# Two-layer graph network on one core: eight node tiles taken by counts in place of seven

## The chip, the cores and the metric

The kernel runs on one core of one Trainium2 chip. The metric is device time of one execution in microseconds (us); the time before is the median of three runs. The core's engines are TensorE (PE; its weight loads are shown apart as PEld), VectorE (DVE), ScalarE (ACT), GpSimd (POOL) and the DMA queues. SP's queue and ACT's queue issue plain DMAs, POOL's queue issues the gathers.

## The reference

Two layers of a graph network over 6250 nodes and 100000 edges, then a residual and a layer norm. The edges are sorted by their destination, and the destinations crowd at low node numbers (6250 times the square of a uniform number), the sources are uniform.

```
x: (6250, 256) f32;  src, dst: (100000,), sorted by dst
agg(h) = (1 + eps) * h + segment_sum(h[src], dst, 6250)
h   = relu(relu(agg(x) @ W1a + b1a) @ W1b + b1b)      # (6250, 512)
y   = relu(agg(h) @ W2a + b2a) @ W2b + b2b            # (6250, 256)
out = layernorm(x + y)
```

## The kernel before, in words

Nodes are cut into 49 tiles of 128, edges into 784 chunks of 128 in the order of their destination. A tile's sum over its edges is made in one of two ways.

**By gathers.** For each chunk POOL issues one indirect DMA (line 461) that fetches the 128 source rows into a piece buffer (early; in layer 2 early and late), with room for 24 chunks in layer 1 and 24 in the two buffers of layer 2. PE sums a chunk onto 32 destination slots with a one-hot matrix sel (L954). Chunks form groups; a group's sums are copied out of their bank by ACT (split, L982 in layer 1, L990 in layer 2), put in place by a matmul with a second one-hot matrix (L1001) and added to the tiles' sums by DVE (acc, L1011). Groups are walked from the highest nodes down.

**By counts.** The lowest tiles have the most edges. For these (HEAVY, seven in both layers) layer 1 makes a table of how often each source occurs for each destination. A chunk's one-hot pair is built by DVE (ca at L1523, cb at L1532), multiplied by PE (L1571) and added to the table `at` at a position taken from the data (L1594). The table holds four tiles at a time (RING) in a ring. Tiles are handled in passes of two, the highest first. When a pass's counts are complete, ACT casts each tile's counts for each range of four source tiles to a matmul operand (cf, L1415), casts them once more to 16-bit integers (ci, L1423) and writes these to DRAM from its own queue (counts, L1428) for layer 2. A pass reads all of x again, 13 ranges of it (raw), in two halves for precision (xh: ACT L1385 and L1392, DVE L1394), and PE multiplies counts with both halves at once, 49 products of 512 columns for each tile (L1457). A ring slot that is used again is cleared by ACT (L1437) first. Layer 2 loads the counts (ci, SP's queue, L1243), casts them (cf, L1255), halves the rows of h1 (upper and xr, L1220, L1221, L1225) and makes two products for each of the 49 source tiles and each counted tile (L1331); DVE adds them up (L1274).

**Dense part.** A block of one or two complete tiles is transposed by PE (L1047), copied to zt by ACT (L1059), multiplied by the layer's first matrix (L1086), passed through a relu by ACT (ht, L1096), and multiplied by the second (L1115). Layer 1 then adds the bias (DVE, L1125), takes a relu (ACT, L1127) and writes h1 to DRAM from ACT's queue (L1128). Layer 2 adds x and the bias, normalizes (L1135 to L1158) and writes the output. The gathers of layer 2 read h1, so the first of them waits for the last write of layer 1.

**What sets the order.** Inside a layer the program is emitted by a planner: an event simulation in Python with a cost for each step, a queue for each of PE, DVE and ACT, and priorities (sums of gathered rows first, the dense part and products after them). Its outcome is a fixed order of instructions on each engine. At run time each engine keeps that order and waits by semaphores. How many tiles are counted, how many chunks, the counting steps, the passes and the groups all follow from HEAVY:

```
HEAVY = (7, 7)
...
NC, taken = counted(N, E, HEAVY[0])
STEPS, END, PASSES, FREE = steps(N, E, taken, HEAVY[0])
NC2 = counted(N, E, HEAVY[1])[0]
groups, lo, hi = (a + b for a, b in zip(places(N, E, NC2, NC), places(N, E, NC, NCH)))
...
assert tiles <= 2 * RING
```

Before both layers, a short part loads the edge lists, derives slots and masks, and tests bounds that the plan assumed about the data. One flag decides between this ordered path and a general one; the times here are of the ordered path.

Of the kernel before, what the change touches and what calls it, by code (L numbers as in the profile page):

```python
# [21 lines left out]
SLOTS = 32  # L22
BURST = 4
PIECES = 6
HEAVY = (7, 7)
RING = 4
W = 10
RANGE = 4
# [39 lines left out]
def counted(N, E, tiles):  # L68

    def node(e):
        return N * min((e + deviation(e, E)) / E, 1.0) ** 2

    total = 0
    while (
        node((total + PARTS) * P) < tiles * P
        and span(N, E, (total + PARTS) * P, P, SIGMAS) <= W
    ):  # L80
        total += PARTS
    taken, at = [], 0
    for n in (8, 4, 2, 1):
        a = at
        while at + n <= total and span(N, E, (at + n) * P, n * P, SIGMAS) <= W:
            at += n
        if at > a:
            taken.append((a, at, n))
    return total, taken


def steps(N, E, taken, tiles):

    def reached(c):
        return N * min((c * P + deviation(c * P, E)) / E, 1.0) ** 2

    def begun(c):
        return N * max((c * P - deviation(c * P, E)) / E, 0.0) ** 2

    todo = sorted(((c, n) for a, b, n in taken for c in range(a, b, n)), reverse=True)  # L100
    end = [
        max(i for i, (c, n) in enumerate(todo) if reached(c + n) >= t * P) for t in range(tiles)
    ]
    passes = [tuple(range(t, max(t - PAIR, -1), -1)) for t in range(tiles - 1, -1, -PAIR)]
    if JOINED and len(passes[-1]) < PAIR:
        passes[-2:] = [passes[-2] + passes[-1]]
    free = [
        next((i for i, (c, n) in enumerate(todo) if begun(c) < ts[-1] * P), len(todo))
        for ts in passes
    ]  # L110
    return todo, end, passes, free


def places(N, E, c, chunks):

    def node(e, side):
        return N * min(max((e + side * deviation(e, E)) / E, 0.0), 1.0) ** 2

    groups, lo, hi = [], [], []
    while c < chunks:
        n = min(GRP, -(-(chunks - c) // PARTS) * PARTS)
        while n > PARTS and (
            span(N, E, (c + n) * P, n // PARTS * P, SPREAD, 1) > SLOTS
            or span(N, E, (c + n) * P, n * P, SPREAD, 1) > P
        ):  # L130
            n -= PARTS
        groups.append((c, n // PARTS))
        lo.append(int(node(c * P, -1)) // P)
        c += n
        hi.append(min(int(node(c * P, 1)), N - 1) // P)
    return groups, lo, hi
# [200 lines left out]
def tile_gin_residual_layernorm(  # L337
# [44 lines left out]
    NCH = -(-E // P)  # L382
# [4 lines that stand above are left out]
    assert NC2 <= NC and HEAVY[1] <= HEAVY[0]  # L387
    groups, lo, hi = (a + b for a, b in zip(places(N, E, NC2, NC), places(N, E, NC, NCH)))
    NG = len(groups)
    BEGIN = (next(g for g in range(NG) if groups[g][0] == NC), 0)  # L390
    SAME = HEAVY[0] == HEAVY[1]
    assert SAME or lo[BEGIN[0]] >= HEAVY[1]
    NCP = groups[-1][0] + PARTS * groups[-1][1]
# [1495 lines left out]
```

## Time and profile before

| | us |
|---|---|
| median of three runs | 1335.6 (1334.89 to 1339.82) |
| the profiled execution's own time | 1333.73 |
| its span, first to last instruction | 1332.0 |
| layer 1, up to the first gather from h | 676.63 |
| layer 2, from there to the end of the span | 655.4 |

The rows of the profile give for a group of instructions the busy time, the mean duration in ns and then the idle time just before them with what ended it. A timeline row gives start, duration, engine, line and the instruction, with its idle time in brackets. A stretch row gives length, busy time by engine with the number of instructions, the granted TensorE clock (1.00 is full), the share of the DMA engines and GB/s. Records of pipelined matmuls overlap, so what a matmul costs is taken from the distance between starts.

### The profile page before, as it was taken

Reading aid. Unit: us, or ns where it says so; the run is one execution under the profiler, and the core shown is the slowest. Engines: PE = TensorE matmul, PEld = TensorE weight load, DVE = VectorE, ACT = ScalarE, POOL = GpSimd, SP = SyncE. Lnnn points to the kernel's source line nnn. Section 1 sums busy time; section 2 is a strip of 40 time slices with the busy share of each in tenths; the row PEclk is TensorE's granted clock in tenths of the full one; section 3 lists DMA queues with packets and bytes.
Section 4 is the critical chain, followed back from the end, with each engine's and each line's share of the span. In section 5 each row is a group of like instructions: output and inputs, shape, how many; then the busy total and the mean of one; then the engine's idle time right before and its main releaser. Section 6 shows DMA issues by size and latency. Waiting matters only on the chain. (4 is left out here: it accounts for less than half of the span.)

```text
span 1332.0 us, 18717 instructions
## 1 busy us (share of the span) xinstructions
PE 1171.7 (88%) x6027; PEld 756.0 (57%) x6027; DVE 872.8 (66%) x2031; ACT 603.2 (45%) x1118; POOL 963.8 (72%) x1002
## 2 busy tenths in 40 slices
PE   2379888999899999878759899999989999999986
PEld 1145554655454655444436667767667766677755
DVE  7689888697897787323127668777756655653443
ACT  0213677767675763454255354334334433432222
POOL 6877777777777777777457677777777777777770
PEclk8589999999999999968879899999989999999999
DMA  3635666667676775566669889888889999877782
GB/s 103 189 119 178 182 219 198 207 199 227 207 225 188 219 239 170 151 211 193 198 228 333 296 268 310 252 278 287 289 271 309 301 310 301 289 244 240 242 244 69
DMA packets 160860, 305.72 MB, mean 230 GB/s; under 512 B 25672, under 2 KB 93150, under 8 KB 160754
## 3 DMA queue, kind: packets, MB, share of 16 engines
q0 software_dynamic: 63232, 194.31, 47.2%
q1 hardware_dynamic: 75110, 84.23, 19.3%
q10 hardware_dynamic: 22412, 25.89, 5.6%
q8 instruction: 51, 0.84, 0.3%
q14 instruction: 55, 0.45, 0.1%
HBM read 273.90 MB, written 30.44 MB: 228 GB/s over the span
## 5 line engine op out<-in xcount | busy, mean ns | idle before, releaser
L461 POOL DMA_INDIRECT early<-in_x_dram,srcs x494 | 488.9, 990 | 158.9 <-issue 127.4
L461 POOL DMA_INDIRECT early<-h,srcs x250 | 239.8, 959 | 101.4 <-issue 58.8
L461 POOL DMA_INDIRECT late<-h,srcs x244 | 232.5, 953 | 77.6 <-issue 60.2
L1011 DVE SCALAR_TENSOR_TENSOR acc<-bank,mask,acc 128x256 f32<-128x256 f32 (+1 forms) x368 | 212.8, 607 | 39.4 <-PE bank L1001 34.8
L1086 PE MATMUL bank<-zt,w2a_s 128*128 128x256 f32 (+2 forms) x864 | 181.8, 366 | 7.7 <-DVE acc L1011 6.5
L1115 PE MATMUL bank<-w1b_s,ht 128*128 128x512 f32 (+1 forms) x392 | 184.7, 599 | 1.1 <-DVE acc L1011 0.8
L1086 PEld LDWEIGHTS bank<-zt,w2a_s 128*128 128x128 f32 x864 | 154.8, 195 | 30.4 <-DVE acc L1011 6.9
L954 PE MATMUL bank<-early,sel 128*32 128x256 f32 (+1 forms) x1488 | 134.3, 475 | 32.7 <-DMA early<-h,srcs 15.3
L1331 PE MATMUL bank<-upper,cf 128*128 128x512 f32 (+1 forms) x343 | 149.2, 435 | 13.9 <-ACT upper L1220 13.5
L1331 PE MATMUL bank<-xr,cf 128*128 128x512 f32 (+1 forms) x343 | 138.2, 403 | 0.8 <-DVE xr L1225 0.8
L1594 DVE TENSOR_TENSOR at<-bank,at 128x490 f32 x174 | 115.9, 666 | 28.2 <-ACT cf L1415 14.7
L907 DVE TENSOR_TENSOR sel<-iota,slot 128x256 f32<-128x256 f32 (+2 forms) x116 | 50.6, 436 | 123.5 <-PE bank L954 119.5
L1086 PE MATMUL bank<-zt,w1a_s 128*128 128x256 f32 (+2 forms) x432 | 103.2, 389 | 13.7 <-ACT zt L1059 10.4
L1001 PE MATMUL bank<-split,to 128*128 128x256 f32 (+2 forms) x340 | 100.0, 415 | 15.6 <-ACT split L987 8.7
L1115 PEld LDWEIGHTS bank<-w1b_s,ht 128*128 128x128 f32 (+1 forms) x392 | 73.3, 191 | 70.8 <-issue 58.6
L1457 PE MATMUL bank<-xh,cf 128*128 128x512 f32 (+1 forms) x343 | 104.1, 440 | 8.7 <-DVE xh L1394 8.6
L1255 ACT CAST cf<-ci 128x512 fp32r<-128x512 uint16 (+1 forms) x91 | 53.8, 595 | 121.4 <-PE bank L1331 104.3
L1096 ACT ACTIVATE ht<-bank,b2a_s 128x256 f32<-128x256 f32 (+2 forms) x108 | 44.6, 451 | 139.5 <-PE bank L1086 137.0
L954 PEld LDWEIGHTS bank<-early,sel 128*32 128x32 f32 x1488 | 40.0, 112 | 113.4 <-issue 80.2
L1571 PE MATMUL bank<-cb,ca 128*128 128x490 f16 x288 | 87.6, 381 | 16.1 <-DVE at L1594 10.5
L1115 PE MATMUL bank<-w2b_s,ht 128*128 128x256 f32 (+1 forms) x392 | 101.5, 390 | 0.0
L1086 PEld LDWEIGHTS bank<-zt,w1a_s 128*128 128x128 f32 x432 | 81.9, 207 | 32.7 <-ACT zt L1059 14.9
(138 smaller groups left out, 1650.7 us busy)
## 6 DMA issues: line engine op xcount, KB each, us to landing
raw<-in_x_dram SPq DMA_DIRECT2D x48, 512.0 KB, 4.5
h<-h1r ACTq DMA_DIRECT2D x48, 256.0 KB, 2.5
xr<-h SPq DMA_DIRECT2D x12, 1024.0 KB, 7.3
counts<-ci ACTq DMA_DIRECT2D x84, 128.0 KB, 3.4
ci<-counts SPq DMA_DIRECT2D x84, 128.0 KB, 5.0
acc<-h SPq DMA_DIRECT2D x19, 512.0 KB, 7.5
early<-in_x_dram,srcs POOLq DMA_INDIRECT x494
acc<-in_x_dram SPq DMA_DIRECT2D x21, 256.0 KB, 3.9
```

What stands on the lines that cost most here:

```text
L461: nc.gpsimd.indirect_dma_start(out=rows_[:, j, :], out_offset=None, in_=table, in_offset=bass.IndirectOffsetOnAxis(ap=srcs[:, c : c + 1], ...
L907: nc.vector.tensor_tensor(sel[:, :n, :], iota[:, :SLOTS].unsqueeze(1).to_broadcast([P, n, SLOTS]), slot[:, c0 : c0 + n].unsqueeze(2).to_br ...
L954: mm = nc.tensor.matmul(pm[b * SLOTS : (b + 1) * SLOTS], sel[:, c - groups[g][0], :], rows_[:, l, :], start=(c == part[0]), stop=(c == par ...
L1001: nc.tensor.matmul(pu[:, i * width : (i + 1) * width], to[:used], split[:used, l, :], start=(once or l == 0), stop=(once or l == 1),)
L1011: nc.vector.scalar_tensor_tensor(acc[t], pu[:, i * width : (i + 1) * width], mask[:, t - lo[g], g : g + 1], acc[t], op0=ALU.mult, op1=ALU.add,
L1086: nc.tensor.matmul(ph[:, (f - o) * TILES * P : (f - o) * TILES * P + nb], wa[:, k, f * P : (f + 1) * P], zt[:, k, :nb], start=(k == 0), st ...
L1115: nc.tensor.matmul(po[:m], ht[:, f, i * P : i * P + m], wb[:, f, :], start=(f == 0), stop=(f == KH - 1),)
L1255: nc.scalar.copy(cf_token.tile[:, :n, :].rearrange("p k j -> p (k j)"), token.tile[:, : n * P],)
L1331: nc.tensor.matmul(bank[token.number][:, :width], cf[:m, j, :], of[:m, j, :], start=(j == 0 and of is upper), stop=(j == len(ks) - 1 and o ...
L1457: nc.tensor.matmul(bank[tokens[i].number][:, : 2 * width], cf[:m, j, :], xh[:m, j, :, :].rearrange("p a d -> p (a d)"), start=(k == 0), st ...
L1571: mm = nc.tensor.matmul(bank[token.number][:, : NT * W], a.tile[:, c % BATCH, :], b.tile, start=(j == 0), stop=(j == n - 1),)
L1594: nc.vector.tensor_tensor(to, bank[token[0].number][:, : NT * W].rearrange("p (k w) -> p k w", w=W), to, op=ALU.add,)
```

## The change

One constant is changed.

```diff
-HEAVY = (7, 7)
+HEAVY = (8, 8)
```

By the kernel's formulas it has these consequences:

| | before | after |
|---|---|---|
| chunks counted, in steps | 288 in 174 | 308 in 194 |
| chunks gathered, each layer | 494 | 474 |
| groups of gathered chunks | 85 | 83 |
| passes of layer 1 | (6,5) (4,3) (2,1) (0) | (7,6) (5,4) (3,2) (1,0) |
| products in layer 1 (L1457) | 343 | 392 |
| products in layer 2 (L1331) | 686 | 784 |
| writes and loads of counts | 91 | 104 |

The ring of four tiles is used exactly twice. The planner is run anew, so the orders of all engines change. The groups of the high tiles and their gathers stay as they were; what changes most is the end of each layer, shown here at three places.

PE at the end of layer 1. Its last gathered sum (L954) and all that stands behind it up to the end of the layer, before; the bank's number is that of a program's buffer:

```order
L954 MATMUL bank_486<-early,sel 32x256 x8
L1001 MATMUL bank_491<-split,to 128x256
L1047 MATMUL bank_493<-ident,acc 128x128 x2
L1047 MATMUL bank_489<-ident,acc 128x128 x2
L1086 MATMUL bank_488<-zt,w1a_s 128x128 x4
L1086 MATMUL bank_492<-zt,w1a_s 128x128 x4
L1086 MATMUL bank_490<-zt,w1a_s 128x128 x4
L1086 MATMUL bank_487<-zt,w1a_s 128x128 x4
L1115 MATMUL bank_486<-w1b_s,ht 128x512 x2
L1115 MATMUL bank_491<-w1b_s,ht 128x512 x2
L1115 MATMUL bank_486<-w1b_s,ht 128x512 x2
L1115 MATMUL bank_491<-w1b_s,ht 128x512 x2
```

After, from the last gathered sum on, the first part of the same place:

```order
L954 MATMUL bank_480<-early,sel 32x256 x4
L1457 MATMUL bank_483<-xh,cf 128x512 x4
L1457 MATMUL bank_484<-xh,cf 128x512 x4
L1001 MATMUL bank_481<-split,to 128x256
L1115 MATMUL bank_485<-w1b_s,ht 128x512 x2
L1047 MATMUL bank_482<-ident,acc 128x128 x2
L1047 MATMUL bank_478<-ident,acc 128x128 x2
L1115 MATMUL bank_485<-w1b_s,ht 128x512 x2
L1457 MATMUL bank_483<-xh,cf 128x512 x4
L1457 MATMUL bank_484<-xh,cf 128x512 x4
L1086 MATMUL bank_479<-zt,w1a_s 128x128 x4
L1086 MATMUL bank_481<-zt,w1a_s 128x128 x4
```

The products L1457 of the last pass were all ahead of the last gathered sum; now 42 of its 98 stand behind it, and behind the last of these the dense part of tiles 0 and 1.

ACT at the same place. From its last copy of a gathered sum (split, L982) on, before:

```order
L982 COPY split<-bank_486 128x256
L1059 COPY zt<-bank_493 128x2x128
L1059 COPY zt<-bank_489 128x2x128
L1096 ACTIVATE ht<-bank_488,b1a_s 128x128 x2
L1096 ACTIVATE ht<-bank_492,b1a_s 128x128 x2
L1096 ACTIVATE ht<-bank_490,b1a_s 128x128 x2
L1096 ACTIVATE ht<-bank_487,b1a_s 128x128 x2
L1127 ACTIVATE h1r<-h1r 128x512
L1128 DMA h_60<-h1r 128x512
L1127 ACTIVATE h1r<-h1r 128x512
L1128 DMA h_60<-h1r 128x512
```

After:

```order
L982 COPY split<-bank_480 128x256
L1096 ACTIVATE ht<-bank_478,b1a_s 128x128
L1415 CAST cf<-at 128x512
L1385 CAST xh<-raw 128x4x256
L1392 COPY bank_479<-raw 128x512
L1423 CAST ci<-cf 128x512
L1428 DMA counts<-ci 128x512
L1415 CAST cf<-at 128x512
L1392 COPY bank_480<-raw 128x512
L1059 COPY zt<-bank_482 128x2x128
L1059 COPY zt<-bank_478 128x2x128
L1423 CAST ci<-cf 128x512
```

The casts, count writes and halvings of the last five ranges now stand behind the last split, mixed with the last tiles' relus.

PE at the end of layer 2. From its last gathered sum on, before (one more row of L1115 closes it):

```order
L954 MATMUL bank_6025<-late,sel 32x512 x4
L1115 MATMUL bank_6029<-w2b_s,ht 128x256 x2
L1001 MATMUL bank_6031<-split,to 128x512 x2
L1047 MATMUL bank_6026<-ident,acc 128x128 x4
L1047 MATMUL bank_6027<-ident,acc 128x128 x4
L1086 MATMUL bank_6028<-zt,w2a_s 128x128 x8
L1086 MATMUL bank_6024<-zt,w2a_s 128x128 x8
L1086 MATMUL bank_6030<-zt,w2a_s 128x128 x8
L1086 MATMUL bank_6025<-zt,w2a_s 128x128 x8
L1115 MATMUL bank_6029<-w2b_s,ht 128x256 x2
L1115 MATMUL bank_6031<-w2b_s,ht 128x256 x2
L1115 MATMUL bank_6029<-w2b_s,ht 128x256 x2
```

After, the first part from the last gathered sum on:

```order
L954 MATMUL bank_6244<-late,sel 32x512 x4
L1115 MATMUL bank_6245<-w2b_s,ht 128x256 x2
L1086 MATMUL bank_6246<-zt,w2a_s 128x256 x8
L1001 MATMUL bank_6241<-split,to 128x512 x2
L1115 MATMUL bank_6245<-w2b_s,ht 128x256 x2
L1115 MATMUL bank_6247<-w2b_s,ht 128x256 x2
L1331 MATMUL bank_6248<-upper,cf 128x512
L1331 MATMUL bank_6248<-xr,cf 128x512
```

Products of the last range (32 of them) and the dense part of several blocks, which stood ahead of the last gathered sum, now stand behind it.

## Prediction

> **What bounds the kernel now.** I read the page's header and engine totals first, then stretches of time cut where the layers meet, then GpSimd's timeline at both layers' last gathers, and last the engines behind those gathers.
>
> ```profile
> span 1332.0 us, 18717 instructions
> PE 1171.7 (88%) x6027; PEld 756.0 (57%) x6027; DVE 872.8 (66%) x2031; ACT 603.2 (45%) x1118; POOL 963.8 (72%) x1002
> 60.00:551.00 491.00, 444.62 (x2218) 258.11 (x2219) 403.15 (x919) 285.43 (x513) 372.56 (x379) 0.97 0.63 194
> 551.00:652.00 101.00, 76.92 (x345) 42.12 (x344) 28.86 (x54) 49.61 (x88) 75.77 (x80) 0.82 0.68 210
> 652.00:677.00 25.00, 18.16 (x91) 9.79 (x90) 4.04 (x9) 8.98 (x19) 0.37 (x1) 0.98 0.23 81
> 677.00:1302.00 625.00, 591.90 (x3163) 421.66 (x3164) 384.79 (x767) 244.46 (x467) 471.49 (x494) 0.97 0.87 282
> 1302.00:1332.00 30.00, 19.40 (x134) 15.15 (x133) 10.00 (x28) 6.67 (x19) 0.45 (x1) 0.93 0.16 52
> ```
>
> The stretches give, after their length, busy time of PE, weight loads, DVE, ACT and POOL, then the granted clock, DMA share and GB/s. POOL's 471.49 of 625 looks like slack and is none:
>
> ```profile
> 630.17 0.94 POOL L461 DMA_INDIRECT early<-in_x_dram,srcs  x1 [0.30 <-issue]
> 650.16 0.95 POOL L461 DMA_INDIRECT early<-in_x_dram,srcs  x1 [0.30 <-issue]
> 676.63 1.13 POOL L461 DMA_INDIRECT early<-h,srcs  x1 [25.53 <-DMA h<-h1r]
> 1301.50 0.95 POOL L461 DMA_INDIRECT late<-h,srcs  x1 [0.30 <-issue]
> ```
>
> The first two are sixteen gathers apart: 19.99/16 = 1.25 us a gather, 0.95 of it busy and 0.30 issue. In layer 2 the 494 gathers take 1301.50 - 676.63 = 624.9 us, 1.265 each, with no stop. So gathers set the pace of both layers, and PE, 591.90 of 625 busy in layer 2, is nearly full beside them. A layer is therefore its gathers times their period, plus what stands behind the last gather. Layer 1 has 26.5 us there (650.16 to 676.63), layer 2 has 30.5 (1301.50 to 1332.0).
>
> **The change, part by part.** Removed: 20 gathers a layer, 20 x 1.25 = 25.0 us in layer 1 and 20 x 1.265 = 25.3 in layer 2. All of it is on the path, and with the last gather gone earlier, the work behind it is late next. Also removed are 20 gathered sums and two groups' merges a layer; they stood at gather pace, and count at nothing, hidden by the gathers that stay.
>
> Added in layer 1: 20 counted chunks (matmul, two builds, an update of the table), a pass that has two tiles in place of one: 49 product matmuls, 13 more table casts, 13 more casts to ci and 13 writes of counts. Per gather the engine order of PE is unchanged up to the last counts: it holds 288 counted chunks up to gather 406 before, and 308 up to gather 430 now. DVE's and ACT's share of it is priced by the rows
>
> ```profile
> L1532 DVE TENSOR_SCALAR cb<-numbers,spot 128x490 f16<-128x490 f16 x288 | 89.4, 352 | 8.4 <-PE bank L1571 8.3
> L1594 DVE TENSOR_TENSOR at<-bank,at 128x490 f32 x174 | 115.9, 666 | 28.2 <-ACT cf L1415 14.7 <-ACT at L1437 7.4 <-PE bank L1571 1.9
> L1523 DVE TENSOR_TENSOR ca<-numbers,low 128x512 f16<-128x512 f16 x72 | 48.8, 678 | 0.0
> L1437 ACT ACTIVATE at<-at 128x512 uint16<-128x512 uint16 x36 | 22.5, 628 | 8.5 <-DVE at L1594 4.0 <-ACT ci L1423 2.8 <-DVE acc L1011 0.4
> ```
>
> 20 x (0.352 + 0.666) + 5 x 0.678 = 23.8 us of DVE, in 30 us more of that stretch: the density of now (403.15 of 491), so it is hidden; 13 clears of the table, 13 x 0.63 = 8 us, lie in ACT's idle time there. If that cover is gone the counts end later still, a us for a us. So the early part runs at gather pace as now, and the last pass begins about 24 x 1.25 = 30 us later, near 582 in place of the 552.37 below, with 44 gathers left in place of 88. It does not fit: of its 98 products 42 now stand behind the last gather, with 20 dense matmuls of 512 columns where 8 stood.
>
> What paces that tail is ACT, which takes its work in order. After its last copy of a gathered sum (split) it had only the last tiles' relus; now it has 10 casts cf, 10 casts ci and 10 count writes, 5 casts xh, 9 copies of raw, 9 relus, 3 h1r and 2 zt before the last pass is through. The prices:
>
> ```profile
> 552.37 0.62 ACT L1415 CAST cf<-at 128x512 fp32r<-128x512 uint16 x1 [0.28 <-DVE at L1594]
> 553.01 0.62 ACT L1423 CAST ci<-cf 128x512 uint16<-128x512 f32 x1
> 553.66 0.33 ACTq L1428 DMA_DIRECT2D counts<-ci  x1
> 554.03 0.62 ACT L1415 CAST cf<-at 128x512 fp32r<-128x512 uint16 x1 [0.40 <-ACT ci L1423]
> L1385 ACT CAST xh<-raw 128x1024 fp32r<-128x1024 f32 x48 | 50.0, 1043 | 5.8 <-ACT ci L1423 2.5 <-PE bank L1457 1.2 <-ACT h1r L1127 1.2
> L1392 ACT COPY bank<-raw 128x512 f32<-128x512 f32 x96 | 55.8, 589 | 20.4 <-DVE xh L1394 6.5 <-DVE at L1594 6.2 <-ACT h1r L1127 3.6
> L1096 ACT ACTIVATE ht<-bank,b1a_s 128x128 f32<-128x128 f32 x20 | 6.4, 363 | 6.1 <-PE bank L1086 5.7 <-ACT h1r L1127 0.4
> L1059 ACT COPY zt<-bank 128x256 f32<-128x256 f32 x6 | 2.2, 372 | 25.6 <-PE bank L1047 18.9 <-DMA ci<-counts 6.7
> 658.71 0.37 ACT L982 COPY split<-bank 128x256 f32<-128x256 f32 x1 [0.40 <-ACT h1r L1127]
> 672.78 0.63 ACT L1127 ACTIVATE h1r<-h1r 128x512 f32<-128x512 f32 x1 [1.09 <-DVE h1r L1125]
> ```
>
> One tile and range costs 554.03 - 552.37 = 1.66 us of ACT, its DMA issue included. Eight of those are 13.3, the two of the short last range an estimated 2.0; xh 4 x 1.04 + 0.4 = 4.6; raw copies 8 x 0.59 + 0.4 = 5.1; relus 9 x 0.36 = 3.3; h1r 3 x (0.63 + 0.4 of issue) = 3.1; zt 0.7: 32 us without a wait. Between that and 42 (ACT often waits for a bank or a raw load here) I take 35, nearer the bottom, because nothing else competes by then. The last gather is issued at 650.16 - 25.0 = 625.2; the split began 8.55 after it (658.71), so now near 633.7, and the last product comes near 633.7 + 0.4 + 35 = 669. From the split to layer 2's first gather it was 676.63 - 658.71 = 17.9: merge, adds, transposes, two matmul stages, relu, write. The last pass is followed by the same chain, for tiles 0 and 1, and I give it 17.9 too. Layer 2 then starts near 687.0 in place of 676.6: **+10.4 for layer 1**. Ends: +3 (PE is free when the last gather lands, some 4 us earlier, and ACT packs closer) and +18 (42 on ACT).
>
> Moved with it: layer 2's first loads.
>
> ```profile
> 631.67 0.37 SPq L710 DMA_DIRECT2D w2a_s<-in_L_gnn_W2a_dram  x1
> ```
>
> They are issued right behind the last raw load and the last product of layer 1, whose buffers they reuse: 45 us ahead of the first gather now, about 18 then. I cost this at nothing: the chain of 17.9 us hides it, with DMA at 0.23 in 652 to 677. If that cover is too short, up to 6 us.
>
> Added in layer 2: 98 product matmuls, 13 loads of counts and 13 casts on ACT (one tile more per range, on an engine busy 244.46 of 625), 13 adds on DVE (384.79 of 625): at nothing, hidden by PE. PE's order is again alike per gather up to the end, so the added work is found at the end: behind the last gathered sum stand 36 matmuls of L1115 (10 before), 24 of L1086 with 256 columns (0 before), 64 with 128 (32 before), 32 products (0 before) and 24 transposes (8 before). Prices, the chain's rows for groups and PE's own last rows:
>
> ```profile
> 759.92 1.85 PE bank L1331 x8
> 787.97 3.45 PE bank L1086 x16
> 886.84 1.73 PE bank L1115 x8
> 1306.62 1.06 PE L954 MATMUL bank<-late,sel 128*32 128x512 f32 x8
> 1311.22 0.66 PE L1047 MATMUL bank<-ident,acc 128*128 128x128 f32 x4 [1.60 <-DVE acc L1011]
> 1312.40 0.66 PE L1047 MATMUL bank<-ident,acc 128*128 128x128 f32 x4 [0.52 <-DVE acc L1011]
> 1312.90 7.31 PE L1086 MATMUL bank<-zt,w2a_s 128*128 128x128 f32 x64
> 1320.04 3.62 PE L1115 MATMUL bank<-w2b_s,ht 128*128 128x256 f32 x16
> ```
>
> Plain f32 matmuls have two records each, products and transposes one. So a product is 1.85/8 = 0.231 us, L1086 3.45/8 = 0.431 with 256 columns and (1320.04 - 1312.90)/32 = 0.223 with 128, L1115 1.73/4 = 0.433, a transpose 0.50/4 = 0.125. The tail grows by 26 x 0.433 + 24 x 0.431 + 32 x 0.223 + 32 x 0.231 + 16 x 0.125 = 11.3 + 10.3 + 7.1 + 7.4 + 2.0 = 38.1 us, against 25.3 saved: **+12.8 for layer 2**. Ends: +9 (PE reaches the last sum 1306.62 - 1301.50 = 5.1 after its issue, partly by its own queue) and +20 (waits such as the 1.60 and 0.52 recur three or four times).
>
> Sum: 10.4 + 12.8 = +23.2 on the profiled execution's 1333.73 us, or 1357. That execution stands 1.9 under the median of 1335.6, within their spread (1334.89 to 1339.82), so I predict 1357 for the new median as well. About 0.5%, 6.7 us, can be told from no change.
>
> **Rivals.**
> (1) The gathers are the whole bound and the tails are hidden: -25.0 - 25.3 gives 1283. The place is PE's queue behind each last gather; it decides if less than 25 us is added there. For it: POOL never stops. Against it: 38 us counted there in layer 2, and PE with 33 us idle in 625.
> A rule gives the same time: the Trainium skill (Perfetto Trace Analysis, Identifying the Most-Contended Engine) says to work on the engine with the highest occupancy and not to judge PE's headroom by matmul busy time but by weight loads. By that rule POOL's 72% stands over the weight loads' 57% and cutting gathers pays in full; the row of 677 to 1302 agrees on POOL alone, not on room behind it.
> (2) ACT keeps pace and PE sets layer 1's end: 12 more dense matmuls at 0.86 (twice L1115's 0.433 for twice the columns), 42 products at 0.231, 8 of L1086 at 0.431 and 4 transposes: 10.3 + 9.7 + 3.4 + 0.5 = 23.9 for 25.0 saved, so -1.1, and 1333.7 - 1.1 + 12.8 = 1345. Against it: 32 us of ACT alone.
> (3) PE runs at a lower clock in the longer tails:
>
> ```profile
> 634.04 2.05 PE L1086 MATMUL bank<-zt,w1a_s 128*128 128x128 f32 x16 [0.46 <-ACT zt L1059]
> 649.25 3.47 PE L1086 MATMUL bank<-zt,w1a_s 128*128 128x128 f32 x16 [5.47 <-ACT zt L1059]
> ```
>
> The same 16 records took 3.47 behind a gap of 5.47 us and 2.05 without it, and the stretch 551 to 652 ran at 0.82. Layer 2's tail of some 52 us at 0.82 would add 11: 1368. Against it: five blocks of independent work keep PE fed there.
> The Trainium skill (TensorE: Matmul & The Clock Gate, HAM oscillation) warns of PE gaps above about 3.4 us, after which the clock is halved; the two rows agree.
> (4) The input breaks one of the bounds that are tested ahead of the branch, and the general path runs. From the input: the highest node among tile 7's counted chunks is 966, under 1023, and a chunk group spans at most 7, under 9. Excluded.
>
> **How the numbers follow.** Forecast 0.71, rival 1 0.05, rival 2 0.14, rival 3 0.10. Summed ends: +3 + 9 = +12 gives 1346, +18 + 6 + 20 = +44 gives 1378; rivals 2 and 3 lie in or beside these. The two ends of every term do not meet often, so 1342 to 1374. Faster by over 0.5%: rival 1, 0.04. Within 0.5%: 0.07, from rival 2 with a shorter layer 2. Slower: 0.89.
>
> **What would show it.** Last gathers 25 us earlier in layer 1 (near 625) and gathers of layer 2 in 600 us; products L1457 until near 669, with ACT busy and PE waiting between 634 and 669; the first gather from h near 687; PE busy for some 50 us behind the last gathered sum, 13 before; no changed period of gathers. I am wrong if the period rises above 1.27, if L1457 ends before 660, or if work behind the last gathers runs ahead of them.

## The result, and the profile after

The changed kernel takes 1366.9 us, the median of four runs (1364.0 to 1369.0), against 1335.9 for the kernel before on the same chip. The ratio, formed from the fast runs of both kernels and not from these two medians, is 1.0245, with a 95% interval of 1.0220 to 1.0270: slower by 31.0 us. The profiled execution took 1369.04 us, 2.1 above its median, where the profiled one of before stood 1.9 under its own; so the two traces differ by 35.1 us, and the working below is of these 35.1.

The head and the engine totals of the changed kernel's page:

```profile
span 1367.1 us, 19005 instructions
PE 1203.0 (88%) x6106; PEld 779.0 (57%) x6106; DVE 899.2 (66%) x2069; ACT 628.7 (46%) x1168; POOL 932.9 (68%) x962
```

The span cut at the changed kernel's own marks: up to the last counts, the last gather, the last products and the first gather from h of layer 1; then up to four us before the last gather of layer 2, and from the last gathered sum almost to PE's last group (the 9 us between these two are not shown; columns as before: length, PE, PEld, DVE, ACT, POOL, clock, DMA share, GB/s):

```profile
60.00:586.00 526.00, 467.82 (x2304) 263.78 (x2304) 427.15 (x969) 294.47 (x531) 399.19 (x401) 0.96 0.62 188
586.00:634.00 48.00, 39.12 (x192) 23.94 (x193) 12.90 (x25) 32.63 (x58) 36.42 (x39) 0.93 0.69 209
634.00:671.00 37.00, 32.67 (x146) 20.35 (x144) 12.46 (x22) 29.28 (x60) 0.47 (x1) 0.95 0.36 118
671.00:694.20 23.20, 13.76 (x36) 8.16 (x36) 2.66 (x7) 4.67 (x8) 0.00 (x0) 0.79 0.58 181
694.20:1294.00 599.80, 566.48 (x2974) 399.32 (x2975) 377.66 (x740) 242.97 (x455) 449.79 (x470) 0.97 0.86 283
1303.00:1357.00 54.00, 51.34 (x300) 45.13 (x300) 20.20 (x53) 13.22 (x35) 0.00 (x0) 0.97 0.11 35
```

The marks themselves, from the timeline, each row with start, duration, engine, line: the last gather of layer 1, the last split, the last products, the load of layer 2's weights, the last write of h, the first gather from h, a wait, the last gather and the last gathered sum.

```profile
633.52 0.95 POOL L461 DMA_INDIRECT early<-in_x_dram,srcs  x1 [0.30 <-issue]
641.36 0.38 ACT L982 COPY split<-bank 128x256 f32<-128x256 f32 x1 [0.40 <-ACT ci L1423]
669.30 1.26 PE L1457 MATMUL bank<-xh,cf 106*128 106x512 f32 x2 [0.30 <-DVE xh L1394]
671.66 0.37 SPq L710 DMA_DIRECT2D w2a_s<-in_L_gnn_W2a_dram  x1
687.59 0.33 ACTq L1128 DMA_DIRECT2D h<-h1r  x1
694.24 1.21 POOL L461 DMA_INDIRECT early<-h,srcs  x1 [59.78 <-DMA acc<-h]
774.93 1.01 POOL L461 DMA_INDIRECT late<-h,srcs  x1 [7.31 <-PE bank L954]
1298.13 0.94 POOL L461 DMA_INDIRECT late<-h,srcs  x1 [0.30 <-issue]
1303.02 1.06 PE L954 MATMUL bank<-late,sel 128*32 128x512 f32 x8
```

The gathers did end sooner: 633.5 in place of 650.2 in layer 1. But GpSimd then waits 59.8 us for h, where it waited 25.5, and in layer 2 PE, which was busy for 19.40 of the 30 us behind the last gather, is now busy for 51.34 of the 54 us behind the last gathered sum. Layer 1 is 17.6 us longer (694.24 - 676.63), layer 2 is 17.5 longer (672.9 - 655.4).

### The profile page after: what moved, and what is told of

Read it like the earlier page. It is cut to its first block, busy times and chain, and to the rows that moved or that the text cites. A ratio compares the mean times of both kernels' runs of the same rounds, so it can differ in the third digit from the quotient of the medians.

```text
span 1367.1 us, 19005 instructions
## 1 busy us (share of the span) xinstructions
PE 1203.0 (88%) x6106; PEld 779.0 (57%) x6106; DVE 899.2 (66%) x2069; ACT 628.7 (46%) x1168; POOL 932.9 (68%) x962
## 5 line engine op out<-in xcount | busy, mean ns | idle before, releaser
L461 POOL DMA_INDIRECT early<-in_x_dram,srcs x474 | 476.6, 1006 | 154.6 <-issue 121.9
L461 POOL DMA_INDIRECT early<-h,srcs x238 | 228.5, 960 | 132.0 <-DMA acc<-h 59.8
L1086 PE MATMUL bank<-zt,w2a_s 128*128 128x256 f32 (+2 forms) x864 | 184.8, 369 | 11.2 <-DVE acc L1011 7.4
L1115 PE MATMUL bank<-w1b_s,ht 128*128 128x512 f32 (+1 forms) x392 | 185.1, 601 | 2.5 <-DVE at L1594 2.2
L1331 PE MATMUL bank<-upper,cf 128*128 128x512 f32 (+1 forms) x392 | 169.8, 433 | 18.6 <-ACT upper L1220 17.7
L1086 PEld LDWEIGHTS bank<-zt,w2a_s 128*128 128x128 f32 x864 | 155.8, 196 | 40.9 <-DVE acc L1011 7.8
L1331 PE MATMUL bank<-xr,cf 128*128 128x512 f32 (+1 forms) x392 | 157.9, 403 | 0.8 <-DVE xr L1225 0.8
L954 PE MATMUL bank<-early,sel 128*32 128x256 f32 (+1 forms) x1424 | 127.6, 473 | 29.5 <-DMA early<-in_x_dram,srcs 10.3
L1594 DVE TENSOR_TENSOR at<-bank,at 128x490 f32 x194 | 129.3, 666 | 29.1 <-ACT cf L1415 12.7
L1457 PE MATMUL bank<-xh,cf 128*128 128x512 f32 x392 | 112.1, 424 | 6.8 <-DVE xh L1394 4.8
L1394 DVE TENSOR_TENSOR xh<-bank,xh 128x512 fp32r<-128x512 f32 (+1 forms) x100 | 67.4, 675 | 72.6 <-ACT bank L1392 72.5
L1115 PEld LDWEIGHTS bank<-w1b_s,ht 128*128 128x128 f32 (+1 forms) x392 | 73.5, 191 | 72.8 <-issue 59.3
L1001 PE MATMUL bank<-split,to 128*128 128x512 f32 (+2 forms) x332 | 96.9, 412 | 12.4 <-ACT split L987 8.4
L1086 PE MATMUL bank<-zt,w1a_s 128*128 128x256 f32 (+2 forms) x432 | 101.1, 383 | 7.3 <-ACT zt L1059 3.7
L1274 DVE TENSOR_TENSOR acc<-bank,acc 128x512 f32<-128x512 f32 x96 | 65.0, 683 | 62.9 <-PE bank L1331 58.3
L1532 DVE TENSOR_SCALAR cb<-numbers,spot 128x490 f16<-128x490 f16 x308 | 95.7, 354 | 8.8 <-PE bank L1571 8.6
```

Of the source, the lines that this page charges most:

```text
L461: nc.gpsimd.indirect_dma_start(out=rows_[:, j, :], out_offset=None, in_=table, in_offset=bass.IndirectOffsetOnAxis(ap=srcs[:, c : c + 1], ...
L954: mm = nc.tensor.matmul(pm[b * SLOTS : (b + 1) * SLOTS], sel[:, c - groups[g][0], :], rows_[:, l, :], start=(c == part[0]), stop=(c == par ...
L1001: nc.tensor.matmul(pu[:, i * width : (i + 1) * width], to[:used], split[:used, l, :], start=(once or l == 0), stop=(once or l == 1),)
L1086: nc.tensor.matmul(ph[:, (f - o) * TILES * P : (f - o) * TILES * P + nb], wa[:, k, f * P : (f + 1) * P], zt[:, k, :nb], start=(k == 0), st ...
L1115: nc.tensor.matmul(po[:m], ht[:, f, i * P : i * P + m], wb[:, f, :], start=(f == 0), stop=(f == KH - 1),)
L1331: nc.tensor.matmul(bank[token.number][:, :width], cf[:m, j, :], of[:m, j, :], start=(j == 0 and of is upper), stop=(j == len(ks) - 1 and o ...
```

## The experiments

The table has the changed kernel and seven edits of it; an eighth edit, of the kernel before, stands at the end of this section. The edits are shown shortened, some with a comment added. Each kernel was timed beside the kernel before on the same chip, so the ratios are what to compare; where intervals overlap, the marks in the traces decide. To read those, the spread is needed: three kernels have the same layer 1 (the changed kernel, and the experiments on the products of ranges 3 to 9 and of range 0 below). Their last products ended at 670.6, 668.0 and 665.7 us and their first gather from h was issued at 694.2, 691.7 and 689.5: means 668.1 and 691.8, and a difference under some 3 us is no effect.

| kernel | ratio to before, 95% interval | last product ends | first gather from h | last gather | from there to the end |
|---|---|---|---|---|---|
| before | 1 | 631.6 | 676.6 | 1301.5 | 30.5 |
| changed | 1.0245 (1.0220 to 1.0270) | 670.6 | 694.2 | 1298.1 | 69.0 |
| eighth tile in layer 1 alone | 1.0110 (1.0079 to 1.0140) | 664.0 | 687.4 | 1312.7 | 40.1 |
| casts on VectorE | 1.0219 (1.0194 to 1.0245) | 664.0 | 687.3 | 1291.7 | 70.4 |
| casts doubled | 1.0271 (1.0246 to 1.0296) | 676.2 | 699.6 | 1303.2 | 68.2 |
| weights loaded behind h | 1.0229 (1.0199 to 1.0258) | 666.3 | 686.4 | 1289.2 | 67.2 |
| 224 products fewer, early | 1.0218 (1.0181 to 1.0255) | 668.0 | 691.7 | 1292.9 | 71.1 |
| 56 products fewer, at the end | 1.0212 (1.0176 to 1.0249) | 665.7 | 689.5 | 1292.4 | 64.0 |
| 19 gathers fewer in layer 1 | 1.0170 (1.0137 to 1.0202) | 657.1 | 680.2 | 1282.5 | 70.8 |

**The eighth tile in layer 1 alone.**

```diff
-HEAVY = (8, 8)
+HEAVY = (8, 7)
```

> The eighth tile in layer 1 alone: HEAVY = (8, 7), layer 2 takes seven tiles by counts and gathers rows for the rest, as before. Theory (the two layers lose separately, each by its own tail): layer 1 as in the changed kernel, its first gather from h near 694 us, and layer 2 as in the kernel before, 655 us from there to the end, so 1347 to 1354 us, about 16 us under the changed kernel. Rival (the loss is one of the boundary: a layer 1 that ends late starts layer 2 badly, whatever its tiles): layer 2 keeps its longer time, 668 us or more, and the whole stays at 1361 us or above. Second rival (only layer 2 costs anything, layer 1's shift is noise of the schedule): 1336 us.

Measured: 1350.1 us, 15.2 above the kernel before and about half of the 31 us. The first gather from h and the last gather (GpSimd's timeline of this kernel):

```profile
687.44 1.03 POOL L461 DMA_INDIRECT early<-h,srcs  x1 [54.52 <-DMA acc<-h]
1312.67 0.97 POOL L461 DMA_INDIRECT late<-h,srcs  x1 [0.30 <-issue]
```

The gathers of layer 2 take 625.2 us, as before (624.9), and none waits for 7 us near 775. The time lay in the range of the first theory, but not by its sum, and so partly by luck: layer 1 came 7 us sooner than in the changed kernel's profile, and layer 2 took 665 us, not 655, since 40.1 us lie behind its last gather and not 30.5. Layer 1 is not quite that of the changed kernel: it casts and writes no counts of tile 7 for layer 2, 13 of each, and its last pass begins at 577.5 us and not at 585.9. So the 15.2 us are not layer 1's alone. With eight tiles grouped for layer 1 and seven counted in layer 2 the groups at the end of layer 2 are cut in another way than before; whether that is the 10 us was not tried. The rival of the boundary (1361 or above) falls, and so does the one by which only layer 2 costs anything (1336).

**ScalarE's casts taken off it, and doubled.** In layer 1's last pass alone:

```diff
-yield ("on", "ACT", act(n * P) + 0.1, 3)
-nc.scalar.copy(ci, ...)
-nc.scalar.dma_start(counts[r, t, :, : n * P], ci)
+yield ("on", "DVE", dve(n * P), 3)
+nc.vector.tensor_copy(ci, ...)
+nc.sync.dma_start(counts[r, t, :, : n * P], ci)
```

> In the last pass of layer 1 the cast of the counts to 16 bits runs on VectorE instead of ScalarE, and the write of the counts is issued from SyncE's queue instead of ScalarE's: 26 casts of 0.65 us and 26 issues of 0.40 us leave ScalarE between 586 and 669 us, some 27 us of its work. Theory (ScalarE paces layer 1's tail): the last product at L1457 ends 4 to 10 us sooner than at 669.3 us, no more because TensorE has 72 us of work in those 85 us; the whole is 1357 to 1363 us. Rival (TensorE paces it, ScalarE only looks busy): the last product ends within 2 us of 669 and the whole is at 1365 us or above.

```diff
+for _ in range(2 if ts == PASSES[-1] else 1):
     nc.scalar.copy(ci, ...)
```

> In the last pass of layer 1 the cast of the counts to 16 bits is issued twice on ScalarE (26 more casts of 0.65 us, 17 us more work for ScalarE between 586 and 669 us; nothing else changes). Theory (ScalarE paces layer 1's tail): the last product ends 8 to 15 us later than 669.3 us, and the whole is 1374 to 1381 us. Rival (TensorE paces it): the extra casts lie in ScalarE's idle time, the last product ends less than 3 us later, and the whole is at 1370 us or below.

PE's group of the products between 586 and 671 us, with its idle time and what ended it, in the changed kernel (and DVE's half of xh over the whole span), then with the casts on VectorE, then with the casts doubled:

```profile
L1457 PE MATMUL bank<-xh,cf 128*128 128x512 f32 (+1 forms) x98 | 30.6, 448 | 4.8 <-DVE xh L1394 2.9 <-ACT cf L1415 1.9
...
L1394 DVE TENSOR_TENSOR xh<-bank,xh 128x512 fp32r<-128x512 f32 x96 | 65.7, 685 | 69.7 <-ACT bank L1392 69.7
```

```profile
L1463 PE MATMUL bank<-xh,cf 128*128 128x512 f32 (+1 forms) x94 | 28.1, 436 | 1.3 <-DVE xh L1394 1.3
```

```profile
L1458 PE MATMUL bank<-xh,cf 128*128 128x512 f32 x87 | 27.2, 436 | 9.6 <-DVE xh L1394 8.4 <-ACT cf L1415 1.1
```

All of DVE's idle time at xh (L1394) ends with a copy by ACT, so both kinds of wait are for ACT in the end. In the changed kernel ACT itself has no pause behind the last split: its row there starts at 641.36 us, its last write of counts is issued at 670.07. Against the mean of the unchanged layer 1, 27 us less on ScalarE bring the last product 4.1 us sooner (664.0, a little outside the spread; the waits for its operands fall from 4.8 to 1.3 us), 17 us more bring it 8.1 us later (676.2). So ScalarE is on the path, and the rival that it only looks busy falls with the second run; but it does not pace the tail alone. With the casts gone PE hardly waits for operands of the products and is still busy for most of the stretch:

```profile
586.00:634.00 48.00, 39.22 (x204) 23.88 (x203) 18.92 (x39) 24.04 (x44) 36.08 (x38) 0.93 0.73 219
634.00:671.00 37.00, 33.51 (x151) 22.28 (x152) 15.31 (x32) 23.32 (x51) 0.00 (x0) 1.00 0.42 139
```

These are 72.7 of the 85 us (71.8 in the changed kernel), the largest wait left, 4.4 us, is for gathered rows, and the products are through at 664. Two engines follow each other closely there. Both effects on the whole time were smaller than expected: 1363.3 us where 1357 to 1363 stood, 1371.1 where 1374 to 1381 stood.

**The weights loaded behind h.** Layer 2's second weights are issued later on SP's queue, behind its first counts:

```diff
-if fetch:
-    fetch()
+def fetching():
+    yield ("rest", 60.0)
+    fetch()
...
+    plan.start(fetching())          # layer 2, behind the first gathers
```

> Layer 2's second weights (1.5 MB in two loads, and a bias) are issued behind the thirteenth load of counts on SyncE's queue, near 719 us, and not at 671.7 us ahead of layer 1's last write of h; they are first used at 754.5 us. Theory (that write lands late because it shares the transfer engines with those loads: 6.65 us from its issue to the first gather from h, 3.2 us before the change): the gap falls to 3 to 4.5 us, the first gather comes near 691.5 us, and the whole is 1362 to 1365 us. Rival (the gap is the write's own, or another load's): within 1 us of the changed kernel's 1366.9 us. Second rival (the later weights hold up layer 2's first dense products): the wait of the gathers near 775 us grows above 7.3 us, and the whole is above 1368 us.

The last write of h, the first gather from it and the load in this kernel's timeline:

```profile
683.23 0.33 ACTq L1128 DMA_DIRECT2D h<-h1r  x1
686.37 1.20 POOL L461 DMA_INDIRECT early<-h,srcs  x1 [54.08 <-issue]
708.26 0.43 SPq L710 DMA_DIRECT2D w2a_s<-in_L_gnn_W2a_dram  x1
```

From the issue of the write to the first gather it is 3.1 us; in the changed kernel it was 6.65 (687.59 to 694.24), in the kernel before 3.2. So 3.5 us of layer 1's loss hang on where these loads stand, and the rival that the gap is the write's own falls. But it is not the weights that the write meets. In the changed kernel's stretches

```profile
674.00:677.00 3.00, 3.00 (x8) 2.35 (x8) 0.00 (x0) 0.00 (x0) 0.00 (x0) 0.50 1.05 398
680.00:683.00 3.00, 3.00 (x9) 1.33 (x7) 0.23 (x1) 0.18 (x1) 0.00 (x0) 1.00 0.13 50
689.00:692.00 3.00, 0.00 (x0) 0.00 (x0) 0.00 (x0) 0.00 (x0) 0.00 (x0) 0.90 0.89 330
```

the transfers have nearly stopped by 680 to 683 us: from 671 to 683 about 2.1 MB were moved, which is what the weights and the small loads behind them amount to. The traffic from 683 on is that of the next loads on SP's queue, 1.5 MB of h that fill acc. Their last two, here and with the weights moved:

```profile
684.43 0.93 SPq L866 DMA_DIRECT2D acc<-h  x2
```

```profile
674.89 0.90 SPq L866 DMA_DIRECT2D acc<-h  x2
```

In the seven kernels of the table with eight tiles in layer 1 and the weights ahead, the last of these loads is issued between 3 us before the last write and 1 us behind it, and the gap is 6.65 to 7.6 us; with the weights moved it is issued 8 us before. The run moved both kinds of load, so that the loads of h are what holds the write is read from the rows and was not tried alone. That the load of the weights came at 708, not 719, changes nothing: PE first uses the weights near 751. The whole went from 31.0 us over the kernel before to 28.8; alone, that would not tell the two apart.

**Fewer products in the middle of layer 2.** This kernel and the next leave out products, as their texts say.

```diff
+halves = (upper,) if 3 <= r <= 9 else (upper, xr)
-for of in (upper, xr):
+for of in halves:
```

> The edit of the earlier run of this kernel once more, since on the chip of that run every kernel, the one before too, took some 300 us longer: layer 2 without 224 of its products (the lower halves, ranges 3 to 9), 53 us of TensorE long before the last gather. Theory (gathers' pace plus tail): layer 2 shortens by no more than the 7.3 us wait near 775 us, its tail stays at 64 us, and the whole is 1360 to 1367 us. Rival (TensorE bounds layer 2): layer 2 at 655 us or less in place of 673, the whole 1349 us or below.

The earlier runs of this kernel and of the next, and the two of the zeroing's sum below, were on a chip that took 1632 us for the kernel before; none of their times is used. A stretch in the middle of layer 2 in the changed kernel and in this one:

```profile
900.00:1100.00 200.00, 194.33 (x1043) 136.87 (x1043) 130.59 (x260) 80.95 (x150) 151.79 (x159) 0.99 0.87 285
```

```profile
900.00:1100.00 200.00, 177.44 (x920) 120.56 (x920) 135.29 (x270) 79.69 (x151) 151.54 (x160) 0.94 0.88 289
```

And this kernel's wait near 775, which now comes at 769:

```profile
768.94 1.03 POOL L461 DMA_INDIRECT late<-h,srcs  x1 [4.25 <-PE bank L954]
```

PE has 123 matmuls less between 900 and 1100 us, and GpSimd's number of gathers is the same (159 and 160). Layer 2 takes 672.3 us (691.7 to 1364.0) in place of 672.9, and the ratio does not move: 1365.1 us, where the first theory had 1360 to 1367 and its rival 1349 or less. Though PE was busy for 194 of 200 us there, its work there cost nothing that shows. (Its busy time fell by 16.9 us only; 123 products at 0.231 would be 28.4. The granted clock was lower too, 0.94 and not 0.99.)

**Fewer products at the end of layer 2.**

```diff
+halves = (upper,) if r == 0 else (upper, xr)
-for j, k in enumerate(ks):
+for j, k in list(enumerate(ks))[: 1 if r == 0 else None]:
```

> The edit of the earlier run of this kernel once more (on the chip of that run every kernel took some 300 us longer): layer 2 makes one product a tile for the last range of source rows in place of eight, 56 products of 0.235 us left out, 13.2 us of TensorE at the end of layer 2, about half of them behind the last gather. Theory (the tail behind the last gather is TensorE's work, and only what lies behind the last gather counts): from the last gather's issue to the end 69.0 us become 60 to 64 us, the last gather stays, and the whole is 1358 to 1362 us. Rival (TensorE bounds the whole layer): all 13 us come off, 1354 us or below. Second rival (the tail is the chain of the dense stage's casts and stores, not the products): 1365 us or above.

The last gathered sum of this kernel (span 1356.4 us):

```profile
1298.93 1.06 PE L954 MATMUL bank<-late,sel 128*32 128x512 f32 x8
```

From the last gather to the end it is 64.0 us, 5.0 less than in the changed kernel and 3 less than in any other here with eight tiles in layer 2; 28 products of 0.231 us, those that stood behind the last sum, are 6.5, and from the last sum to the end it is 57.5 us where the changed kernel has 64.1: 6.6 less. The whole was expected at 1358 to 1362 and is 1360.8. The pair of runs is the answer for layer 2: 53 us of PE's work in the middle are free, and of 13 us at the end those behind the last gather come off.

**Fewer gathers in layer 1.** Nineteen are left out; the sums take what stood there.

```diff
 for j, (c, b) in enumerate(pieces[number][i][1])
+if not (number == 1 and j == 3 and 20 <= i <= 110 and i % 5 == 0)
```

> The changed kernel without 19 of layer 1's gathers, spread over the layer (the fourth of every fifth piece from 20 to 110; the sums then take what stood in that place), 19 x 1.25 = 23.8 us of the gathers' pace; the order on all other engines is unchanged. Theory (layer 1's end follows from its last gather, its split and 35 us behind it, as the prediction's sum has it): the last gather of layer 1 comes near 610 us, the first gather from h 20 to 24 us sooner than 694.2 us, and the whole is 1343 to 1348 us. Rival (the gathers set the pace no longer; the last counts at 584 us and the products of ScalarE and TensorE behind them set the end): the first gather from h moves by less than 6 us, the whole is 1361 to 1367 us. Between them (the counts stand in TensorE's order among the sums, so they too come sooner, but not by all): the last counts move as far as the end does.

```profile
192.70 0.94 POOL L461 DMA_INDIRECT early<-in_x_dram,srcs  x1 [4.34 <-PE bank L955]
620.29 0.95 POOL L461 DMA_INDIRECT early<-in_x_dram,srcs  x1 [0.30 <-issue]
```

All gathers of layer 1 as one group (count, busy time, mean ns, idle time and what ended it), in this kernel, then in the changed one, then in the kernel before:

```profile
L461 POOL DMA_INDIRECT early<-in_x_dram,srcs x455 | 456.3, 1003 | 161.7 <-issue 117.6 <-PE bank L955 23.4 <-DVE rawf L535 5.5
```

```profile
L461 POOL DMA_INDIRECT early<-in_x_dram,srcs x474 | 476.6, 1006 | 154.6 <-issue 121.9 <-PE bank L954 8.6 <-DVE rawf L534 5.7
```

```profile
L461 POOL DMA_INDIRECT early<-in_x_dram,srcs x494 | 488.9, 990 | 158.9 <-issue 127.4 <-PE bank L954 7.2 <-DVE rawf L534 5.5
```

Both named theories miss, and the time lies between them; the case named there, that the last counts move as far as the end, does not hold as it stands. The last counts come before the last pass, which begins at 578.7 us, 7.2 before that of the changed kernel's profile and 5.5 before the mean of the three kernels with the unchanged layer 1 (585.9, 585.0, 581.6); the first gather from h moved by 14.0 and 11.6. The 23.8 us moved the last gather by 13.2 against the changed kernel's profile (620.3 against 633.5) and by 10.9 against that mean (633.5, 631.3, 628.7), the time by 8.3 (22.7 over the kernel before, 31.0 for the changed kernel). What is missing went to waits like the one at 192.70: the gathers wait 23.4 us for sums by PE (line 955 in this kernel), 14.8 more than in the changed one. So in layer 1 gathers and PE are close to each other, and a gather taken away gave about half its period.

**The zeroing of the table.** The gathers beside its seven zeroings are long. First the memset as a sum, in the changed kernel and in the kernel before:

```diff
-nc.vector.memset(at[:, k : k + 7, :].bitcast(mybir.dt.uint32), 0)
+nc.vector.tensor_tensor(here, none, none, op=ALU.add)   # none: a zero operand
```

> The changed kernel with its seven zeroings of the count table (L1541, 1.58 us each, between 37 and 69 us) written as a sum of two zero operands on VectorE in place of a memset: about 2.5 us each by the rate of the sums at L1594 (0.666 us for 490 elements), and by the trace no such sum stretches a gather. The seven gathers beside the memsets took 17.4 us together, against 0.945 us each in the undisturbed stretch; they should fall to about 7 us, and the last gather of layer 1 come near 623.5 us in place of 633.5. Theory (layer 1's end follows from its last gather, split and 35 us behind it, as the prediction's sum has it): the first gather from h comes 8 to 10 us sooner and the whole is 1356 to 1360 us. Rival (layer 1's end follows from the last counts at 584 us and the work of ScalarE and TensorE behind them, and the gathers are no longer on its path): the gathers end 10 us sooner and the first gather from h moves by less than 3 us, the whole is 1363 us or above.

> The kernel before with the same edit of the seven zeroings. Theory (in the kernel before, layer 1 ends with its gathers, so what shortens a gather shortens the layer): the last gather of layer 1 comes 9 to 11 us sooner than 650.2 us and the whole is 1323 to 1328 us. Rival (the long gathers beside the memsets have another cause, the full startup of the transfer queues): no change, 1334 to 1336 us.

Their times are not used, for the reason above, but the rows still show what stretches a gather. A sum and the gather beside it, in the kernel before with this edit:

```profile
54.74 2.06 DVE L1545 TENSOR_TENSOR at<-zero 128x1827 f32<-128x1827 f32 x1
```

```profile
54.76 3.45 POOL L463 DMA_INDIRECT early<-in_x_dram,srcs  x1 [0.30 <-issue]
```

The gather is as long as beside a memset, so the memset is not special, and the expectation that sums leave gathers alone was wrong. Then on ScalarE, in the kernel before:

```diff
+nc.scalar.copy(here, none)
```

> The kernel before with its seven zeroings of the count table on ScalarE (copies of a zero operand, 1827 words each) in place of memsets on VectorE. In the earlier run the gathers beside the zeroings stayed long (1.7 to 3.5 us) when the memset was written as a sum on VectorE, so it is not the memset but any long VectorE instruction. Theory (a long VectorE instruction holds back the gather's issue on GpSimd, and layer 1 of the kernel before ends with its gathers): the seven gathers fall from 17.4 us together to about 7, the last gather of layer 1 comes 5 to 10 us sooner than 650.2 us, and the whole is 1325 to 1331 us. Rival (ScalarE's first splits come 3 to 5 us later behind the copies and the gathers wait for their buffers instead): 1333 to 1338 us. Second rival (the long gathers stay, whichever engine zeroes): 1334 to 1336 us.

The kernel before (a memset and the gather beside it), then this one (its copies run from 54.59 to 68.01 us; the first row is the longest gather beside them):

```profile
44.77 1.58 DVE L1541 MEMSET at<- 128x1827 uint32 x1 [0.33 <-issue]
...
44.63 3.07 POOL L461 DMA_INDIRECT early<-in_x_dram,srcs  x1 [0.30 <-issue]
```

```profile
64.06 1.24 POOL L463 DMA_INDIRECT early<-in_x_dram,srcs  x1 [0.30 <-issue]
73.76 0.94 POOL L463 DMA_INDIRECT early<-in_x_dram,srcs  x1 [3.36 <-PE bank L956]
```

The long gathers are gone: layer 1's gathers are busy for 7.1 us less (481.8 against 488.9). But they wait 7.2 us more for PE's sums (14.4 against 7.2), and the last gather stays, at 650.46. The ratio is 1.0001 (0.9980 to 1.0022), so the theory's 1325 to 1331 us misses. The rival holds: ScalarE's first splits come 4.5 us later behind the copies (56.19 against 51.74), PE waits 13.6 us for one of them in place of 8.7, and 1333.2 us is the edge of its 1333 to 1338. No version that was run beats the kernel before.

## Why the prediction was right, and where its sum was not

The side, the cause (what stands behind each layer's last gather) and the range were right; the sum of +23.2 was too small against +35.1 between the profiles, 31.0 between the medians. Layer 1 was forecast at +10.4 and came to +17.6, by errors of +7.7, -7.5 and +7.0 in its three steps; layer 2 at +12.8 and +17.5, mostly by one of 4.3. That the total stayed in the range owes something to the -7.5. By its steps:

- **"20 gathers a layer ... all of it is on the path", -25.0 in layer 1.** This term was mis-sized: the last gather came 16.6 us sooner (650.16 to 633.52), or 19 by the mean of the three kernels with this layer 1. The run with 19 gathers fewer shows one kind of loss: where gathers get fewer, they wait for PE's sums. In the changed kernel itself these waits are only 1.4 us more than before (8.6 and 7.2 in the groups' rows above); nearly all of the rest is that a gather takes 1006 ns in the mean and not 990, 7.6 us over 474. In the other two kernels with this layer 1 the mean is 1000 and 999 ns, so a part of this is spread. In the trace 42 of the gathers take over 1.1 us, 32 before; the added ones stand mostly beside VectorE's building of the count table (ca and cb), of which there is more now. No run tried whether that is the cause.
- **The last product near 669, paced by ACT.** It started at 669.30, which is luck: two errors stand against each other. The last split came at 641.4 and not 633.7, and the work behind it took 28 us, not 35. This work is the prediction's list to the last item (ten casts of each kind, five xh, nine copies of raw, nine relus, three h1r, two zt), but it ran without a pause, where 3 us were allowed for waits, and the sum of durations, 32 us, was itself too long: such a row of ACT starts about 0.1 us before the row ahead ends, so that its price is the distance between starts, as for PE (the first row here ends at 643.46):

```profile
642.40 1.06 ACT L1385 CAST xh<-raw 128x1024 fp32r<-128x1024 f32 x1
643.35 0.60 ACT L1392 COPY bank<-raw 128x512 f32<-128x512 f32 x1
```

That ACT sets this pace is half right: more work for ACT costs about half of itself, and less brings 4 us before other waits hold. Rival 2, 1345 by PE alone, has layer 1 end 1.1 us sooner than before; with the casts off ScalarE the first gather from h still comes 10.7 us later (687.3 against 676.6), some 4 of them beyond the two losses of the next step, so its sum for PE is too small, and the doubled casts speak against its condition.
- **The chain of 17.9 to the first gather from h.** It took 24.9 (669.30 to 694.24). 3.5 come with the load of the weights, which the prediction set at nothing, up to 6; the failed reason is that the chain "hides" it. The weights themselves are hidden, but the loads of h that follow them on the queue are late by it and are moved together with the last write of h. Some 3 are the dense part, 15.9 us from transposes to write (671.73 to 687.59) and not 13.0 (660.41 to 673.44 in the kernel before): its sixteen records of L1086 with 256 columns took 5.62 us, 3.65 in layer 2's tail (these rows). The granted clock was 0.50 from 674 to 677 us, 0.79 over the whole chain; in the kernel before it was 1.00 from 661 to 671. The clock of rival 3 was thus met here, in the short chain, and not where that rival had its 11 us: layer 2's tail ran at 0.97. That rival's 1368 is the forecast nearest to the measured 1366.9, but by chance.

```profile
671.73 1.11 PE L1047 MATMUL bank<-ident,acc 128*128 128x128 f32 x4 [1.18 <-DVE acc L1472]
673.52 5.78 PE L1086 MATMUL bank<-zt,w1a_s 128*128 128x256 f32 x16 [0.68 <-ACT zt L1059]
679.14 7.03 PE L1115 MATMUL bank<-w1b_s,ht 128*128 128x512 f32 x16
1299.37 3.72 PE L1086 MATMUL bank<-zt,w2a_s 128*128 128x256 f32 x16
```

The kernel before at the same place:

```profile
660.41 0.83 PE L1047 MATMUL bank<-ident,acc 128*128 128x128 f32 x4 [0.58 <-DVE acc L1011]
...
673.44 0.33 ACTq L1128 DMA_DIRECT2D h<-h1r  x1
```

- **Layer 2's tail, +38.1.** From the last gathered sum to the end it is 64.1 us (1303.02 to 1367.1), 25.4 before: +38.7. The sum over the engine's order, each kind of matmul at its own price, was right to 2%, and the two runs with fewer products show that only this place counts.
- **Layer 2's gathers, -25.3, the added work hidden.** They took 603.9 us, 21.0 less. The missing 4.3 is a term that was left out: the wait near 775 us is 7.31 where it was 3.08 (the row below). The other kernels with eight tiles counted in layer 2 have it too, 5.48 to 7.99 us, and 4.25 with fewer products; the one with eight tiles in layer 1 alone has none over 2 us there. So it goes with the eighth tile in layer 2; which part of that tile's work makes it was not tried. The period outside this wait is 596.6/473 = 1.261 us.

```profile
753.36 1.01 POOL L461 DMA_INDIRECT late<-h,srcs  x1 [3.08 <-PE bank L954]
```

- **Rival 1, 1283.** Its condition (less than 25 us added behind a last gather) was not met in layer 2, where 38.7 were. The Trainium skill's rule that gives the same time (Perfetto Trace Analysis, Identifying the Most-Contended Engine) points to GpSimd here, and GpSimd's gathers do end sooner; the time does not follow.

## What to carry to other kernels

When work moves from the pacing engine to another, price what then stands behind the last instruction of the pace, from the order of the engine that has to do it: that sum was within 2% here, while the average share of an engine (PE at 194 of 200 us busy) told nothing of its cost. Do not book the whole saving of the pacing engine where a second one is nearly as full: in layer 1, with PE at 468 of 526 us, between half and three quarters came through. And at a boundary, look for bulk loads that are issued just ahead of the one small write that all wait for, and for what delays these loads on their queue.

## What the runs showed of the hardware

- A gather issued on GpSimd beside a memset or a sum of 1827 elements on VectorE is done only after that instruction: 3.07 us beside a memset of 1.58, 3.45 beside a sum of 2.06, at most 1.24 beside the same zeroing on ScalarE. All seven gathers beside the memsets end 0.95 to 1.4 us after the memset does, and an undisturbed one takes 0.95: it is held back until VectorE is through. The Trainium skill (SBUF — State Buffer, SBUF: two separate sides) describes the ports that the two engines share as an exclusive lock, held for the whole instruction. For the length of the hold the rows agree; but as VectorE's takers of the lock the section names instructions in a 2-port mode or with two SBUF inputs, and the memset, which has no input, held the gather all the same. Whether it ran in such a mode no run shows.
- The last write of h in layer 1, 256 KB, is issued 2 to 4 us behind 1.5 MB of loads on another queue, and its reader starts 6.65 us later; where these loads are issued 8 us ahead or more, it is 3.1 to 3.2. All of them had been issued when the write was. That they are what delays it was not tried alone.
